# One-hots moved to VectorE and maxima spread with fewer products, in a graph attention layer on one core

## The chip, the cores and the metric

The kernel runs on one NeuronCore of one Trainium2 chip. The metric is the device time of one execution in microseconds (us), the median over several runs; lower is better. The engines have their own instruction streams, which meet at semaphores: PE (TensorE, matrix products, whose weight loads the profile lists as PEld), DVE (VectorE), ACT (ScalarE), POOL (GpSimd) and SP (SyncE, used here to start DMAs). Each executes its instructions in the order of the program.

## What is computed

A layer of relational graph attention with 5 relations, 8 heads of 16 and 3125 nodes of 128 features, over 100,000 edges that come sorted by their destination, followed by two residual layer norms. Cut to what matters:

```python
for r in range(R):                                   # R = 5 relations
    mask = edge_types == r
    q = einsum('eh,khd->ekd', x[dst], W_Q[r])
    k = einsum('eh,khd->ekd', x[src], W_K[r])
    v = einsum('eh,khd->ekd', x[src], W_V[r])
    logits = (q * k).sum(-1) / 4 + attn_bias[r]
    masked = where(mask, logits, -1e9)
    max_v = maximum(segment_max(masked, dst), -1e9)
    exp_l = where(mask, exp(masked - max_v[dst]), 0)
    sum_exp = segment_sum(exp_l, dst)
    attn = exp_l / (sum_exp[dst] + 1e-12)
    out = out + segment_sum(attn[:, :, None] * v, dst)
h = layernorm(x + out @ out_proj_w.T + out_proj_b)   # with gamma and beta
return layernorm(x + h)                              # without
```

The maximum of each node, relation and head must be known before the exponentials of that node's edges, which is what gives the kernel its two passes over the edges.

## The kernel before

**Tiles.** The edges are cut into 196 groups of 512 edges (`NGR`, `GE`): T = 4 tiles of 128 edges, one edge to a partition. Because the edges are sorted, the destinations of a group fall into a window of 25 nodes, that is WR = 125 pairs of node and relation.

**Before the loop** the keys and values of all nodes and relations are computed and stored to a table in DRAM (`kv_d`), the queries to another (`q_d`, written as three bf16 parts whose sum is the float32 value), and the indices are prepared.

**The loop** runs over steps k. An edge group passes it twice. On its first pass it is called g, one group a step from step 0 to 195:

- `gather(g)` (L681): four indirect DMAs issued by POOL fetch the key and value rows of the 512 edges from `kv_d` into one of 21 row buffers (`KVB`; group g overwrites group g - 21). It is issued two steps ahead (`AHEAD`). The gathers of groups 0 to 8 are issued before the loop.
- `fetch_keys`, `fetch_q` (L367, L373, SP): the keys `kt` of the edges' destinations, and the window's queries `qw`.
- `spot(g)` (L738): one tensor_scalar compares `kt` with the partition's number and writes the one-hot matrix `hot`, 125 x 512 in bf16. It stands two steps ahead of the group's own step. It runs on POOL, except for groups 0 and 1, which run on DVE.
- `spread_q(g)` (L747, PE): 12 products (4 tiles, 3 parts) with `hot` as weights bring each edge its query row, in PSUM.
- `logits(g)` (L760, L761, DVE): keys times queries, summed over each head; `store_logits` (L766, SP) writes them to DRAM.
- The logits of full blocks of 128 nodes are fetched again by one gather of POOL (`maxima_load`, L773, every eighth step), and `maxima` (L796 to L832, DVE, three steps in a row) takes the maximum of each node, relation and head. The result is again written as three bf16 parts, to `m_d`.

On its second pass, 16 to 19 steps later, the group is called v:

- `fetch_m(v)` (L854, SP): the maxima of the window, `mw`, 125 rows of 2 halves x 3 parts x 4 heads.
- `spread_m(v, times)` (L864, PE): 12 products with the same `hot` bring each edge the maxima of its destination, adding the three parts in PSUM. The row of maxima is repeated `times` times in each product, 8 while there are still gathers and 12 in the last 19 steps; only the first copy is read.
- `less_max(v)` (L873, DVE): logits less maxima, in place in PSUM (`mde`). `exps` (L877, ACT): the exponentials, in place. `weigh(v)` (L882, DVE): values times weights to `wv`, read from the row buffer and `mde`; `weights` (L890, ACT) copies the weights beside them.
- `places` (L902, L905, ACT): a second matrix `at` of 0 and 1, by destination.
- `sums(v, done)` (L916, L918, L925, PE): sums over the edges of each node and relation, with what the group before has left of a shared window (`carry`, L931, ACT), and, for a group two steps older, the sum over the relations (`by_node`, L950, ACT).
- `norm(v)` (L937 to L940, DVE): division by the sum of the weights.

Every block of 128 nodes then passes the output projection and the two norms (L957 to L1008).

**The order** is written out by hand in the loop of L1063 to L1155. Within a step DVE executes weigh(v) of the step, then `less_max` of the next group, `norm` of the group two steps older, `logits(g)`, then (for groups 0 and 1) `spot`, then queries and maxima, then the norms of nodes. POOL executes the four gathers of group k + 2, the gather of maxima when one is due, then `spot` of group k + 2. PE executes `spread_m` of the next group, `sums`, then `spread_q` of the next group. The `hot` tiles live in 21 buffers, `mw` in 4, `me` and `qe` in 2 banks of PSUM each.

Of the kernel before, what the change touches and what calls it, by code (L numbers as in the profile page):

```python
# [8 lines left out]
F32 = mybir.dt.float32  # L9
# [3 lines left out]
ALU = mybir.AluOpType  # L13
AX = mybir.AxisListType
# [3 lines left out]
P = 128  # L18
# [4 lines left out]
HEADS = 8  # L23
# [17 lines left out]
T = GE // P  # L41
# [5 lines left out]
WR = WN * R  # L47
# [67 lines left out]
def block_of(g, ends=tuple(P * (b + 1) for b in range(NT))):  # L115

    return min(
        b for b, n in enumerate(ends)
        if n >= N or E // N * n - slack(n) >= min(E, (g + 1) * GE)
    )  # L120
# [12 lines left out]
def windowed_path(  # L133
# [4 lines left out]
    nc = tc.nc  # L138
# [90 lines left out]
    def iota(name, pattern, n, base=0, mult=0, dt=F32, pool=const):  # L229
        t = pool.tile([P, n], dt, name=name)  # L230
        nc.gpsimd.iota(
            t, pattern=pattern, base=base, channel_multiplier=mult,
            allow_small_or_imprecise_dtypes=True,
        )
        return t

    node = iota("node", [[P, NT]], NT, mult=1)
    row_of = iota("row_of", [[0, 1]], 1, mult=1)
# [113 lines left out]
    live = {}  # L352
# [12 lines left out]
    def fetch_keys(g):  # L365
        kt = ahead.tile([P, T, P], BF16, name="kt")
        nc.sync.dma_start(kt.rearrange("w t p -> w (t p)"), key_d[g].partition_broadcast(P))  # L367
        live["kt", g] = kt

    def fetch_q(g):  # L370
        qw = ahead.tile([P, 3, H], BF16, name="qw")
        f = window(g, first5, SPE)
        nc.sync.dma_start(qw.rearrange("w s h -> w (s h)"), q_d[bass.ds(f, P), :])  # L373
        live["qw", g] = qw
# [298 lines left out]
    ps = ctx.enter_context(tc.tile_pool(name="ps", bufs=2, space=PSUM))  # L673
    buffers(i for i in range(KVB) if i not in at_once)
    hold = ctx.enter_context(tc.tile_pool(name="hold", bufs=HELD))
    flow = ctx.enter_context(tc.tile_pool(name="flow", bufs=2))
# [10 lines left out]
    def fetch_x(name, b):  # L687
        n = min(P, N - b * P)
        xb = flow.tile([P, H], F32, name=name, bufs=2 if name == "xq" else 3)
        if n < P:  # L690
            nc.vector.memset(xb, 0.0)
        nc.sync.dma_start(xb[:n], x[b * P : b * P + n, :])
        live[name, b] = xb
# [26 lines left out]
    def second_part():  # L720
        rem, q3 = live["rem"]
        nc.scalar.copy(q3[:, :, 1, :], rem)
# [5 lines left out]
    def store_q(b):  # L728
        live.pop(("xT", b))
        nc.sync.dma_start(  # L730
            q_d[b * P * R : (b + 1) * P * R, :].rearrange("(p r) c -> p (r c)", r=R),
            live.pop(("q3", b)).rearrange("p r s h -> p (r s h)"),
        )

    def spot(g):
        hot = hold.tile([WR, T, P], BF16, name="hot")
        on = nc.vector if g < 2 else nc.gpsimd
        on.tensor_scalar(hot, live.pop(("kt", g))[:WR], row_of[:WR], None, op0=ALU.is_equal)  # L738
        live["hot", g] = hot

    def spread_q(g):
# [109 lines left out]
    def fetch_m(g):  # L851
        mw = late_flow.tile([P, 2, 3, HEADS // 2], BF16, name="mw", bufs=4)
        f = window(g, first5, SPE)
        nc.sync.dma_start(mw.rearrange("w h s k -> w (h s k)"), m_d[bass.ds(f, P), :])  # L854
        live["mw", g] = mw


    def spread_m(g, times):

        me = ps.tile([P, T, times, 2, HEADS // 2], F32, name="me", tag="me")  # L860
        hot, mw = live.pop(("hot", g)), live.pop(("mw", g))
        for t in range(T):
            for s in range(3):
                nc.tensor.matmul(  # L864
                    me[:, t], hot[:, t, :],
                    mw[:WR, None, :, s, :].to_broadcast([WR, times, 2, HEADS // 2]),
                    start=(s == 0), stop=(s == 2),
                )
        live["mde", g] = me[:, :, 0].rearrange("p t h k -> p t (h k)")

    def less_max(g):
        mde = live["mde", g]
        nc.vector.tensor_tensor(mde, live.pop(("lg", g))[:, :, :HEADS], mde, op=ALU.subtract)  # L873

# [73 lines left out]
    def by_node(g):  # L948
        f = window(g, first, ACTE)
        nc.scalar.copy(oT[:, bass.ds(f, WN)], live.pop(("op", g)))  # L950
# [18 lines left out]
    def residual(b):  # L969
        n = min(P, N - b * P)  # L970
        if ("mv", b) not in live:
            live["mv", b] = pair()
            nc.vector.memset(live["mv", b], 0.0)
        xb = live["xr", b]
        nc.vector.tensor_tensor(xb[:n], xb[:n], beta_t[:n], op=ALU.add)
        h = late_flow.tile([P, H], F32, name="h", bufs=3)
        nc.vector.tensor_tensor(h[:n], live.pop(("pj", b))[:n], xb[:n], op=ALU.add)
        moments(live["mv", b][:, 0, :], h[:n], n)
        live["h", b] = h
# [34 lines left out]
    def store_z(b):  # L1014
        n = min(P, N - b * P)
        nc.sync.dma_start(out[b * P : b * P + n, :], live.pop(("z", b))[:n, :])
# [6 lines left out]
    group_at = {k: g for g, k in step_of.items()}  # L1023
# [10 lines left out]
    at_k, k = {}, 0  # L1034
    for v in range(NGR):
        k = max(k + 1, ready[block_of(v, MEND)])
        at_k[v] = k
    v_at = {k: v for v, k in at_k.items()}
# [24 lines left out]
    for k in range(-2, root_at[NT] + 2):  # L1063
        v, g = v_at.get(k), group_at.get(k)
        q_step = {k - f: b for b, f in enumerate(q_from) if b >= QB and -2 <= k - f <= 5}

        if k >= 0 and k + 3 in group_at:
            fetch_keys(group_at[k + 3])
            fetch_q(group_at[k + 3])
        if -2 in q_step:  # L1070
            fetch_x("xq", q_step[-2])
        for b in range(NT):
            if done_at[b] - 1 == k:
                fetch_x("xr", b)
            if norm_at[b + 1] + 1 == k:
                store_z(b)
        if 5 in q_step:
            store_q(q_step[5])
        for u in range(NGR):
            if max(at_k[u] - 3, ready[block_of(u, MEND)] - 2) == k:  # L1080
                fetch_m(u)

        for b in range(NT):
            if done_at[b] + 1 == k:
                residual(b)
        if v_at.get(k - 4) is not None:
            by_node(v_at[k - 4])
        if v_at.get(k - 2) is not None:
            carry(v_at[k - 2])
        if 1 in q_step:  # L1090
            turned(q_step[1])
        if 3 in q_step or 4 in q_step:
            second_part()
        if 2 in q_step or 3 in q_step:
            first_part()

        if v_at.get(k + 1) is not None:
            spread_m(v_at[k + 1], 8 if k + 1 in group_at else 12)
        if v_at.get(k - 1) is not None or v_at.get(k - 3) is not None:
            sums(v_at.get(k - 1), v_at.get(k - 3))  # L1100
        if k + 1 in group_at:
            spread_q(group_at[k + 1])

        if v is not None:
            weigh(v)
        while gathered < NGR - 1 and step_of[gathered + 1] <= k + AHEAD:
            gathered += 1
            gather(gathered)
        for b in range(NM):
            if full_step[b] + 1 == k:  # L1110
                maxima_load(b)
        if v_at.get(k + 1) is not None:
            less_max(v_at[k + 1])
            exps(v_at[k + 1])
        if v is not None:
            weights(v)
        if k + 1 in group_at:
            types(group_at[k + 1])
        if v_at.get(k - 2) is not None:
            norm(v_at[k - 2])  # L1120
        if g is not None:
            logits(g)
            store_logits(g)
        if k + 2 in group_at:
            spot(group_at[k + 2])
        if v_at.get(k + 1) is not None:
            places(v_at[k + 1], 2 if k >= final - 1 else 0)
        if 3 in q_step or 4 in q_step:
            third_part()
        if 2 in q_step or 3 in q_step:  # L1130
            remainder()
        for b in range(NM):
            whole = MB[b][2] is None
            last = ready[b] - (3 if whole else 4)
            if last - 2 == k and whole:
                maxima(b, 0, 2)
            if last - 1 == k and whole:
                maxima(b, 2, 4)
            if last == k:
                maxima(b, 4 if whole else 0, R)  # L1140
                store_m(b)
        for b in range(NT):
            if done_at[b] == k:
                project(b)
        for b in range(NT + 1):
            if root_at[b] == k:
                roots(b)
            if norm_at[b] == k:
                norms(b)
        if 0 in q_step:  # L1150
            turn_q(q_step[0])
        if 1 in q_step:
            queries(q_step[1], 0, RH)
        if 2 in q_step:
            queries(q_step[2], RH, R)  # L1155
# [505 lines left out]
```

## Time and profile before

| | us |
|---|---|
| runs | 1504.70, 1506.07, 1506.73 (median 1506.07) |
| the profiled execution | 1506.07 |
| its span (first to last instruction) | 1504.3 |
| busy in the span: PE, DVE, ACT, POOL | 1005.8, 901.7, 637.9, 1123.9 |

The mean granted clock of PE is 0.686 of full speed. What the program does when: the setup up to 93 us, gathers of POOL from 93.1 to 1419.1 with the loop, and the last steps, without gathers, to 1504.3.

How to read it: a line of a timeline gives the start in us, the duration in us, the engine, the source line, the operation with output and inputs, how many instructions run together, and in brackets the idle time of the engine ahead of it with what ended it. A line of the groups gives the busy time and mean duration in ns, then the idle time ahead of the group with its main cause; "issue" is time in which the engine waited for nothing that the profile shows. A line of the slices gives the busy share in tenths for each fortieth of the span. A line of the windows gives a stretch, its length, the busy time and count for PE, PEld, DVE, ACT and POOL, then the granted clock, the share of the DMA engines that was busy, and GB/s.

### The profile page before, as it was taken

Reading aid. Unit: us, or ns where it says so; the run is one execution under the profiler, and the core shown is the slowest. Engines: PE = TensorE matmul, PEld = TensorE weight load, DVE = VectorE, ACT = ScalarE, POOL = GpSimd, SP = SyncE. Lnnn points to the kernel's source line nnn. Section 1 sums busy time; section 2 is a strip of 40 time slices with the busy share of each in tenths; the row PEclk is TensorE's granted clock in tenths of the full one; section 3 lists DMA queues with packets and bytes.
Section 4 is the critical chain, followed back from the end, with each engine's and each line's share of the span. In section 5 each row is a group of like instructions: output and inputs, shape, how many; then the busy total and the mean of one; then the engine's idle time right before and its main releaser. Section 6 shows DMA issues by size and latency. Waiting matters only on the chain.

```text
span 1504.3 us, 26147 instructions
## 1 busy us (share of the span) xinstructions
PE 1005.8 (67%) x7526; PEld 800.1 (53%) x7526; DVE 901.7 (60%) x2365; ACT 637.9 (42%) x2248; POOL 1123.9 (75%) x1095
## 2 busy tenths in 40 slices
PE   7961336576676767667677677666776767667775
PEld 3530235455565645556565555555655555556664
DVE  5531446366557666656756665665765665566486
ACT  2540123344444454544544454444445444444354
POOL 2446788888888888888888888888888888888600
PEclk9975556566566677666767766767666776755688
DMA  6873544554554554455555545455545545444300
GB/s 184 317 255 96 143 132 122 141 139 119 146 135 128 141 139 127 132 148 128 126 146 136 127 140 140 122 145 138 135 125 144 137 125 142 130 132 120 98 17 16
DMA packets 180892, 203.66 MB, mean 135 GB/s; under 512 B 83207, under 2 KB 146083, under 8 KB 180620
## 3 DMA queue, kind: packets, MB, share of 16 engines
q0 software_dynamic: 40896, 113.39, 26.5%
q1 hardware_dynamic: 135414, 83.80, 22.7%
q10 hardware_dynamic: 4430, 4.71, 1.3%
q8 instruction: 63, 1.03, 0.3%
q14 instruction: 89, 0.73, 0.2%
HBM read 166.50 MB, written 35.28 MB: 134 GB/s over the span
## 4 chain that ended last, share of the span: by engine, by line
POOL 36%; PE 26%; issue 15%; DVE 11%; DMA 7%; another core or an unknown queue 2%; SPq 1%; ACT 1%; DVEq 0%; POOLq 0%; ACTq 0%
POOL kv L681 22%; POOL hot L738 14%; PE qe L747 6%; PE pp L916 6%; PE me L864 5%; DMA kv<-kv_d,idx 5%; PE pr L395 3%; DVE lg L761 2%; DVE prod L760 1%; PE prq L707 1%; PE pp L918 1%; PE pp L925 1%; DMA mw<-m_d 1%; POOL ell L773 1%
## 5 line engine op out<-in xcount | busy, mean ns | idle before, releaser
L681 POOL DMA_INDIRECT kv<-kv_d,idx x784 | 761.4, 971 | 227.6 <-issue 172.0
L747 PE MATMUL qe<-qw,hot 125*128 125x128 bf16 x2352 | 248.9, 283 | 435.1 <-POOL hot L738 393.1
L747 PEld LDWEIGHTS <-hot 125*128 125x128 bf16 x2352 | 202.8, 130 | 461.1 <-POOL hot L738 424.1
L916 PE MATMUL pp<-wv,at 128*125 128x136 f32 x1568 | 407.1, 402 | 0.0
L916 PEld LDWEIGHTS pp<-wv,at 128*125 128x125 f32 x1568 | 312.3, 272 | 69.4 <-issue 69.1
L738 POOL TENSOR_SCALAR hot<-kt,row_of 125x512 bf16<-125x512 bf16 x194 | 308.9, 1592 | 14.3 <-DMA kt<-key_d 8.4
L873 DVE TENSOR_TENSOR me<-lg,me 128x32 f32<-128x32 f32 x196 | 38.3, 195 | 357.0 <-PE pp L916 135.5
L877 ACT ACTIVATE me<-me 128x32 f32<-128x32 f32 x196 | 35.7, 182 | 486.2 <-issue 332.2
L902 ACT ACTIVATE at<-row_at,nkey 128x125 f32<-128x125 f32 x744 | 237.5, 398 | 0.0
L760 DVE TENSOR_TENSOR prod<-kv,qe 128x512 f32<-128x512 f32 x196 | 132.9, 678 | 63.5 <-PE qe L747 25.4
L864 PE MATMUL me<-mw,hot 125*128 125x64 bf16 (+1 forms) x2352 | 149.3, 229 | 24.9 <-DMA mw<-m_d 14.9
L864 PEld LDWEIGHTS <-hot 125*128 125x128 bf16 x2352 | 137.0, 123 | 51.5 <-issue 36.5
L882 DVE TENSOR_TENSOR wv<-kv,me 128x512 f32<-128x512 f32 x196 | 132.8, 677 | 23.2 <-remote 14.0
L761 DVE TENSOR_REDUCE lg<-prod 128x32 f32<-128x512 f32 x196 | 134.4, 686 | 6.7
L905 ACT ACTIVATE at<-at 128x500 f32<-128x500 f32 (+1 forms) x196 | 117.3, 599 | 6.2
L918 PE MATMUL pp<-pt,carried 125*5 125x136 f32 x390 | 100.7, 351 | 1.1 <-ACT pt L931 0.9
L811 DVE TENSOR_TENSOR wl<-by_head,shut 128x1024 f32<-128x1024 f32 (+2 forms) x73 | 76.9, 1053 | 12.7 <-ACT by_head L788 10.2
L925 PEld LDWEIGHTS pp<-rsum,o 125*128 125x128 f32 x392 | 80.9, 250 | 4.2 <-issue 4.1
L817 DVE TENSOR_REDUCE mx<-wl 128x16 f32<-128x1024 f32 (+2 forms) x73 | 76.5, 1048 | 2.5
L925 PE MATMUL pp<-rsum,o 125*128 125x25 f32 x392 | 71.6, 266 | 4.0 <-DVE o L940 4.0
L950 ACT COPY oT<-pp 128x25 f32 x196 | 33.8, 172 | 86.4 <-remote 32.1
L395 PE MATMUL pr<-wkv,xT 128*128 128x512 f32 x150 | 60.8, 547 | 3.6 <-issue 3.1
(185 smaller groups left out, 987.3 us busy)
## 6 DMA issues: line engine op xcount, KB each, us to landing
kt<-key_d SPq DMA_DIRECT2D x196, 128.0 KB
qw<-q_d SPq DMA_DIRECT2D x196, 96.0 KB
kv_d<-kvs SPq DMA_DIRECT2D x24, 640.0 KB
kv<-kv_d,idx POOLq DMA_INDIRECT x784
q_d<-q SPq DMA_DIRECT2D x22, 480.0 KB
lg_d<-lg SPq DMA_DIRECT2D x196, 18.0 KB
mw<-m_d SPq DMA_DIRECT2D x196, 6.0 KB
xr<-in_x SPq DMA_DIRECT2D x24, 64.0 KB
```

The lines of the kernel that those rows point to most:

```text
L681: nc.gpsimd.indirect_dma_start(out=kv[:, t, :], out_offset=None, in_=kv_d[:, :], in_offset=bass.IndirectOffsetOnAxis(ap=idx[:, t, g : g + ...
L738: on.tensor_scalar(hot, live.pop(("kt", g))[:WR], row_of[:WR], None, op0=ALU.is_equal)
L747: nc.tensor.matmul(qe[:, t, :], hot[:, t, :], qw[:WR, s, :], start=(s == 0), stop=(s == 2))
L760: nc.vector.tensor_tensor(prod, kv[:, :, :H], live.pop(("qe", g)), op=ALU.mult)
L761: nc.vector.tensor_reduce(lg[:, :, :HEADS], prod.rearrange("p t (k d) -> p t k d", d=HD), AX.X, ALU.add)
L864: nc.tensor.matmul(me[:, t], hot[:, t, :], mw[:WR, None, :, s, :].to_broadcast([WR, times, 2, HEADS // 2]), start=(s == 0), stop=(s == 2),)
L882: nc.vector.tensor_tensor(wv[:, :, :H].rearrange("p t (k d) -> p t k d", d=HD), kv[:, :, H:].rearrange("p t (k d) -> p t k d", d=HD), live ...
L902: nc.scalar.activation(at[:, t, :], row_at[:, :WR], AF.Abs, bias=nkey[:, t, g : g + 1], scale=1.0)
L905: nc.scalar.activation(at[:, on_dve:], at[:, on_dve:], AF.Relu, bias=1.0, scale=-1.0)
L916: nc.tensor.matmul(pp, at[:, t, :], wv[:, t, :], start=(t == 0), stop=(t == T - 1))
L918: nc.tensor.matmul(pp[:R], carried[:WR, g, :], live.pop(("pt", g - 1)), start=False, stop=False,)
L925: nc.tensor.matmul(op, live.pop(("o5", done)), rsum[:WR], start=True, stop=True)
```

## The change

Two things are changed. All of `spot` runs on DVE. And while there are gathers, `spread_m` issues one product for each of the four tiles instead of three: the three parts stand side by side in the product's columns, repeated 5 times (5 x 24 = 120 columns), and `less_max` first adds the three parts with a tensor_reduce on DVE into a new tile in SBUF, which the subtraction, the exponentials, `weigh` and `weights` then use in place of PSUM. In the last 19 steps the 12 products stay.

```diff
     def spot(g):
         hot = hold.tile([WR, T, P], BF16, name="hot")
-        on = nc.vector if g < 2 else nc.gpsimd
-        on.tensor_scalar(hot, live.pop(("kt", g))[:WR], row_of[:WR], None, op0=ALU.is_equal)
+        nc.vector.tensor_scalar(hot, live.pop(("kt", g))[:WR], row_of[:WR], None, op0=ALU.is_equal)
         live["hot", g] = hot

     def spread_m(g, times):

+        hot, mw = live.pop(("hot", g)), live.pop(("mw", g))
+        if times < 8:
+            me = ps.tile([P, T, times, 2, 3, HEADS // 2], F32, name="me", tag="me")
+            for t in range(T):
+                nc.tensor.matmul(
+                    me[:, t], hot[:, t, :],
+                    mw[:WR, None].to_broadcast([WR, times, 2, 3, HEADS // 2]),
+                    start=True, stop=True,
+                )
+            live["parts", g] = me[:, :, 0].rearrange("p t h s k -> p t h k s")
+            return
         me = ps.tile([P, T, times, 2, HEADS // 2], F32, name="me", tag="me")
-        hot, mw = live.pop(("hot", g)), live.pop(("mw", g))
         for t in range(T):
             for s in range(3):
                 nc.tensor.matmul(
...
     def less_max(g):
+        if ("parts", g) in live:
+            mde = flow.tile([P, T, 2, HEADS // 2], F32, name="mde")
+            nc.vector.tensor_reduce(mde, live.pop(("parts", g)), AX.X, ALU.add)
+            live["mde", g] = mde.rearrange("p t h k -> p t (h k)")
         mde = live["mde", g]
         nc.vector.tensor_tensor(mde, live.pop(("lg", g))[:, :, :HEADS], mde, op=ALU.subtract)
...
         if v_at.get(k + 1) is not None:
-            spread_m(v_at[k + 1], 8 if k + 1 in group_at else 12)
+            spread_m(v_at[k + 1], 5 if k + 1 in group_at else 12)
```

## The prediction

> **What bounds the kernel now.** I read the busy shares and the slices first, then the costliest groups, then the timeline of one stretch of POOL, then the windows by stage.
>
> ```profile
> PE 1005.8 (67%) x7526; PEld 800.1 (53%) x7526; DVE 901.7 (60%) x2365; ACT 637.9 (42%) x2248; POOL 1123.9 (75%) x1095
> POOL 2446788888888888888888888888888888888600
> ```
>
> ```profile
> L681 POOL DMA_INDIRECT kv<-kv_d,idx x784 | 761.4, 971 | 227.6 <-issue 172.0
> L747 PE MATMUL qe<-qw,hot 125*128 125x128 bf16 x2352 | 248.9, 283 | 435.1 <-POOL hot L738 393.1
> L738 POOL TENSOR_SCALAR hot<-kt,row_of 125x512 bf16<-125x512 bf16 x194 | 308.9, 1592 | 14.3 <-DMA kt<-key_d 8.4
> L873 DVE TENSOR_TENSOR me<-lg,me 128x32 f32<-128x32 f32 x196 | 38.3, 195 | 357.0 <-PE pp L916 135.5
> ```
>
> POOL is the busiest engine and flat at 8 tenths from slice 8 to the end of the loop; PE's largest wait is for POOL's hot. The stretch of POOL shows why it is not 10 tenths:
>
> ```profile
> 198.67 1.00 POOL L681 DMA_INDIRECT kv<-kv_d,idx  x1 [0.17 <-issue]
> 199.97 0.97 POOL L681 DMA_INDIRECT kv<-kv_d,idx  x1 [0.31 <-issue]
> 201.25 0.95 POOL L681 DMA_INDIRECT kv<-kv_d,idx  x1 [0.30 <-issue]
> 202.51 0.95 POOL L681 DMA_INDIRECT kv<-kv_d,idx  x1 [0.30 <-issue]
> 203.49 1.59 POOL L738 TENSOR_SCALAR hot<-kt,row_of 125x512 bf16<-125x512 bf16 x1
> 205.25 1.00 POOL L681 DMA_INDIRECT kv<-kv_d,idx  x1 [0.17 <-issue]
> ```
>
> The 0.3 us between gathers is issue, no wait. From the first gather of one step to that of the next: 205.25 - 198.67 = 6.58 us. Every eighth step a gather of maxima (L773) adds 0.96 + 0.31 = 1.27, or 0.16 a step: 6.74. Gathers 0 to 8 are issued before the loop; the train of gather 9 starts at 157.9, and 157.9 + 187 x 6.74 = 1418.3, against 1419.1 read for the end of the last gather. So POOL's program is the whole time to there; the drained pipeline behind it takes 85 us. The profiled execution is 1506.07 (span 1504.3, 1.8 around it), which is the median of the runs too, so the sum needs no shift.
>
> The stage windows bound the other engines:
>
> ```profile
> 600.00:1000.00 400.00, 279.18 (x2200) 228.22 (x2197) 251.43 (x659) 188.31 (x660) 331.43 (x304) 0.68 0.53 136
> 1420.00:1504.00 84.00, 56.65 (x512) 45.88 (x512) 62.27 (x231) 37.42 (x151) 2.96 (x3) 0.81 0.09 20
> ```
>
> In 400 us, 59.3 steps of 6.74: PE 4.71 us a step at a granted clock of 0.68, DVE 4.24, ACT 3.17.
>
> **A second thing that POOL does to the loop.** Two pairs of lines, the first from the steady part, the second from the end, where no gathers run:
>
> ```profile
> 766.70 0.85 PE L864 MATMUL me<-mw,hot 125*128 125x64 bf16 x12
> 769.13 0.20 DVE L873 TENSOR_TENSOR me<-lg,me 128x32 f32<-128x32 f32 x1 [3.15 <-PE pp L916]
> ...
> 1452.40 0.68 PE L864 MATMUL me<-mw,hot 125*128 125x96 bf16 x12 [0.36 <-DMA mw<-m_d]
> 1453.18 0.20 DVE L873 TENSOR_TENSOR me<-lg,me 128x32 f32<-128x32 f32 x1 [0.59 <-PE me L864]
> ```
>
> DVE is idle in both, yet its subtraction begins 769.13 - 767.55 = 1.6 us after the last product of maxima in the first (median over the loop 1.6) and 0.1 in the second. So PE's finished signals come late while a train of four gathers is issued; many of them come together some 0.9 us after the last gather of a train, that is, during the hot. Before the loop, where gathers run back to back with no hot between, it is far worse:
>
> ```profile
> 105.63 2.72 PE L747 MATMUL qe<-qw,hot 125*128 125x128 bf16 x24 [1.47 <-issue]
> ...
> 118.58 0.69 DVE L760 TENSOR_TENSOR prod<-kv,qe 128x512 f32<-128x512 f32 x1 [12.79 <-issue]
> ...
> 143.77 0.69 DVE L760 TENSOR_TENSOR prod<-kv,qe 128x512 f32<-128x512 f32 x1 [23.78 <-remote]
> ```
>
> The products of groups 0 and 1 are done at 107.1 and 108.35; their consumers start at 118.6 and at 143.8, 5 us after the last gather of that train (its last began at 137.49). The cause of the delay isn't visible, its size is.
>
> **The change, part by part.**
>
> *The hot moves from POOL to DVE.* POOL loses 194 instructions; a step's train becomes 4 x 1.26 = 5.04 us (137.49 - 136.23 = 1.26 in the run without hots), with maxima 5.20: 1.54 us less a step. On DVE the same instruction took 353 and 456 ns in its two cases (groups 0 and 1), 0.36 from start to start at most; bounds 0.2 (the small tensor_scalar L806, median 194 ns) and 1.59 (POOL's own price). I take 0.36, the same instruction. It issues no DMA. On DVE it stands behind logits(k), which waits for qe(k), and ahead of the maxima, queries and weigh(k+1); PE's spread_q(k+2) and, sixteen or so steps later, spread_m wait for it. It no longer waits for POOL's train, so the 393.1 us that PE idles for it go.
>
> The Trainium skill ("SBUF — State Buffer", Who interferes with whom) has a rule against this: a tensor_scalar on DVE in a two-port mode locks the port pair that it shares with GpSimd, and whoever issues second waits in full. The row that bears on it is L806, a tensor_scalar run beside the gathers, at 182 to 490 ns; by the rule 187 hots of 0.36 us would give 67 us back to POOL, which I leave out of the sum.
>
> *The spread in 4 products.* 12 products of 64 columns (L864 mean 229 ns, a group of 12 taking 0.52 us warm and 0.85 cold from start to end) become 4 of 120 columns; nearest row L747, 128 columns, 283 ns: a third of a 12-group that takes 0.84 to 1.46, so 0.28 to 0.49. PE gets 0.25 to 0.35 us shorter a step in 177 steps and issues 56 instead of 72 matmuls and weight loads. PE isn't the bound, so this is worth nothing on the path by itself: its cover is the 435.1 us of idle ahead of L747. If that cover goes, it is worth the 0.3. Its other side is the clock: less work may keep the clock at half. At half clock the step's products take 0.49 + 1.70 + 0.6 + 0.82 + 0.46 + 1.46 = 5.5 us.
>
> *The sum of three parts.* One tensor_reduce of 96 elements a partition more on DVE, 32 out; bounds L873 (195 ns, 32 elements) and L761 (686 ns, 512 elements); 96 is nearer to 32, so 0.2, ahead of the subtraction, and thus on the chain me, less_max, exps, weigh. PSUM's me is free once it is summed, instead of after weigh and weights: no wait for it shows now, so nothing.
>
> DVE comes to 4.24 + 0.36 + 0.20 = 4.8 us a step, under 5.20.
>
> *Where the stall goes.* gather(k+2) overwrites the rows that weigh(k) reads (21 buffers, group g over g-21). Now weigh ends 1.6 to 29 us before the gather that it lets go, 5.8 at the median. At 1.54 us saved a step, that reserve is spent within four steps; from there POOL waits for weigh. Weigh waits for exps, they for less_max, it for a signal of PE, and that signal comes late in a train. Without the hot there is no gap behind a train, so POOL runs two trains (one has its weigh done already), stops, and only this stop lets PE's signals through. The stop: 0.9 us until the signals come, then DVE's chain from less_max through norm and logits to the end of weigh, 763.25 to 765.98 in the timeline, 2.73 us: together 3.6 for two trains, 1.8 a step. Bounds: 0.9 + 0.68 (weigh alone behind the signal) = 1.6, or 0.8 a step; and 3.6 + 0.56 (hot and sum) + 1.35, or 2.75 a step. (1.35: DVE's 4.24 less the 2.89 that its seven instructions of every step take by their rows leaves 1.35 a step for maxima, queries and norms, 2.7 in two steps, of which I let half fall into the stop.) I take 1.8: in the lines above less_max itself is what comes late.
>
> **Sum of the forecast.** Gathers 9 to 20 overwrite nothing: 12 steps at 5.20 instead of 6.74, -18.5. The other 175 go at 5.20 + 1.80 = 7.00 instead of 6.74: +45.5. 1506.1 - 18.5 + 45.5 = 1533 us. With a stop of 1.55 a step, 1489; with 2.45, 1647: that is its own range.
>
> **Rivals.**
> 1. *POOL bounds as it does now, and gets shorter.* For: the flat slices, and the reserve ahead of each gather. Against: the two consumers that started 11.5 and 35 us late. 157.9 + 187 x 5.20 = 1130, + 85 + 1.8: 1217; with DVE or a cold PE as the bound (5.5 us a step) 1273.
> 2. *A short stop.* The signal of maxima comes at the end of the third gather, as at 769.13, since now 8 instead of 24 instructions of PE stand behind it; behind the stop comes weigh alone. 0.8 a step: 6.0, 1367; 1.35 a step, 6.55, 1470. For: 16 instructions fewer to be signalled. Against: without the gap, 24 products were enough for the delay of 11.5 us.
> 3. *Slower*, my forecast's mechanism: place, the lack of a gap behind each train; price, the stop; it decides from a stop of 1.64 us a step, where -18.5 + 175 x (5.20 + stop - 6.74) is zero. At the upper bound of 2.75 it gives 1506.1 - 18.5 + 175 x 1.21 = 1699.
> 4. *The hot on DVE takes what it took on POOL*, 1.59: DVE at 6.03 a step, 1372. No row on DVE comes near.
>
> **How the numbers follow.** The forecast's case 0.56 (slower 0.50, within 0.03, faster 0.03), the short stop 0.27 (faster 0.24, within 0.02, slower 0.01), POOL, DVE or PE as the bound 0.15, the rest 0.02, slower. About 0.2% is what a measurement of this kernel can tell from no change. Faster 0.42, same 0.05, slower 0.53. The likeliest time is 1533. For 8 in 10 the range leaves out the POOL-bound case and the top of the stop: 1367 to 1650.
>
> **What would show it.** Right: gathers in pairs of trains with a stop of 3 to 4 us before the third, first gather of a pair released by weigh (L882); L873's place taken by the reduce, waiting on PE with 2 us and more between me's last product and it; L738 on DVE at 0.36. Wrong: trains without stops at 5.04, or stops under 2 us; a reduce that starts 0.1 us after its products; hots on DVE of over 1 us, or gathers whose 0.96 grows beside them.

## The result, and the profile after

| | before | after |
|---|---|---|
| median, us | 1506.3 (1504.7 to 1506.7) | 1556.8 (1549.2 to 1564.8) |
| ratio | | 1.034 (95% interval 1.028 to 1.039) |
| profiled span, us | 1504.3 | 1551.9 |
| granted clock of PE | 0.686 | 0.708 |

The change makes the kernel 3.4% slower. 1533 was forecast, in a range of 1367 to 1650. In what follows a *train* is the four gathers of one group, a *row* is what POOL issues without a stop, and a *stop* is a wait of POOL ahead of a train. First the page of the profile after: the busy times, POOL's slices, and the groups that answer to those shown of before (idle time and its main cause behind the last bar; "remote" is a wait whose end the profile can put down to no instruction of this core).

```profile
PE 912.1 (59%) x6110; PEld 690.0 (44%) x6110; DVE 972.3 (63%) x2736; ACT 648.0 (42%) x2248; POOL 808.4 (52%) x901
POOL 2556354464655655565565566556556455555500
...
L681 POOL DMA_INDIRECT kv<-kv_d,idx x784 | 753.5, 961 | 552.3 <-DVE mde L883 302.2
L746 PE MATMUL qe<-qw,hot 125*128 125x128 bf16 x2352 | 230.8, 260 | 107.5 <-issue 63.2
L883 DVE TENSOR_REDUCE mde<-me 128x32 f32<-128x96 f32 x177 | 44.7, 253 | 260.2 <-remote 146.6
```

POOL has lost 315 us of work and is no longer flat. PE has lost nearly all of its wait for the hot. In their place POOL waits 302 us ahead of gathers. DVE waits 260 us ahead of the sum of the maxima, where it waited 357 us ahead of the subtraction before. The windows, with the columns as before (PE, PEld, DVE, ACT, POOL, clock, DMA share, GB/s):

```profile
600.00:1000.00 400.00, 234.16 (x1660) 180.45 (x1658) 269.70 (x760) 185.54 (x644) 228.54 (x238) 0.72 0.52 131
...
1465.00:1551.00 86.00, 61.49 (x538) 49.85 (x535) 66.89 (x244) 40.61 (x164) 5.20 (x6) 0.80 0.11 24
```

No engine is over 68% busy in the middle: the engines wait for each other. What they wait for shows in the timeline. First PE's products and the consumer on DVE at the end of a row of gathers that ran from 683.36 to 699.72 with no stop (POOL's lines are further down):

```profile
692.45 0.44 PE L746 MATMUL qe<-qw,hot 125*128 125x128 bf16 x5
693.39 0.39 PE L746 MATMUL qe<-qw,hot 125*128 125x128 bf16 x2 [0.50 <-issue]
694.09 0.27 PE L746 MATMUL qe<-qw,hot 125*128 125x128 bf16 x1 [0.32 <-issue]
694.81 0.38 PE L746 MATMUL qe<-qw,hot 125*128 125x128 bf16 x2 [0.46 <-issue]
696.22 0.37 PE L746 MATMUL qe<-qw,hot 125*128 125x128 bf16 x2 [1.02 <-issue]
...
701.25 0.26 DVE L883 TENSOR_REDUCE mde<-me 128x32 f32<-128x96 f32 x1 [9.97 <-remote]
```

The twelve products are one group, which in the kernel before takes 0.84 us where the granted clock is 1.0 and 1.46 where it is 0.5. Here, after the first five, they drip out one or two at a time, 0.7 us or a multiple of it apart, with nothing that the profile shows to wait for. The products that this sum reads were done at 688.1 (their group starts at 687.74 and takes 0.37), and the sum begins at 701.25, 1.5 us after the last gather. So the row of gathers delays PE's signals, as the prediction said, and in the end PE's own instructions too, which it had not said. Of the groups of queries from group 14 on, 18 of 182 took over 1.8 us, up to 8.0; before, none took over 1.46. From group 52 on all 15 of these are eight groups or a multiple of eight apart, so they keep to the eight-step round of the maxima; which part of that round sets them off isn't shown.

The same round on POOL:

```profile
683.36 0.95 POOL L681 DMA_INDIRECT kv<-kv_d,idx  x1 [3.49 <-DVE mde L883]
...
698.77 0.95 POOL L681 DMA_INDIRECT kv<-kv_d,idx  x1 [0.30 <-issue]
706.31 0.95 POOL L681 DMA_INDIRECT kv<-kv_d,idx  x1 [6.59 <-DVE mde L883]
...
713.06 0.95 POOL L681 DMA_INDIRECT kv<-kv_d,idx  x1 [2.05 <-DVE mde L883]
```

A row of three trains, then a stop of 6.6 us, then single trains with stops of 1 to 2 us (a gather of maxima at 693.77 stands within the row). Each gather behind a stop starts 0.27 us after the end of the weigh that freed its buffer (the profile names the instruction next to it, L883); 109 of the 175 trains from group 21 on start within 0.5 us of that weigh, before none.

Last, the start, where no buffer has to be waited for:

```profile
155.35 0.69 DVE L759 TENSOR_TENSOR prod<-kv,qe 128x512 f32<-128x512 f32 x1 [31.87 <-remote]
...
223.09 0.69 DVE L759 TENSOR_TENSOR prod<-kv,qe 128x512 f32<-128x512 f32 x1 [28.34 <-remote]
```

```profile
150.53 0.94 POOL L681 DMA_INDIRECT kv<-kv_d,idx  x1 [0.30 <-issue]
175.97 0.94 POOL L772 DMA_INDIRECT ell<-lg_d,start_i  x1 [24.50 <-DMA kt<-key_d]
...
244.51 0.95 POOL L772 DMA_INDIRECT ell<-lg_d,start_i  x1 [22.60 <-DVE mde L883]
```

POOL gathers in two long rows, which end at 151.5 and 221.9; DVE stands still for 32 and 28 us, until 3.9 and 1.2 us after the end of each row; then POOL stands still for 24.5 and 22.6 us, since its next instruction, the gather of maxima (L772), needs the logits that DVE couldn't compute in the meantime.

### The profile page after: what moved, and what is told of

It reads as the page before. It is cut to its first block, busy times and chain, and to the rows that moved or that the text cites. A ratio compares the mean times of both kernels' runs of the same rounds, so it can differ in the third digit from the quotient of the medians.

```text
span 1551.9 us, 22874 instructions
## 1 busy us (share of the span) xinstructions
PE 912.1 (59%) x6110; PEld 690.0 (44%) x6110; DVE 972.3 (63%) x2736; ACT 648.0 (42%) x2248; POOL 808.4 (52%) x901
## 4 chain that ended last, share of the span: by engine, by line
DVE 32%; PE 21%; another core or an unknown queue 16%; issue 15%; DMA 5%; ACT 5%; SPq 3%; POOL 1%; DVEq 0%; ACTq 0%; POOLq 0%
PE pp L929 7%; DVE prod L759 4%; DVE wv L895 4%; DVE wl L810 4%; DVE lg L760 4%; PE qe L746 3%; DMA mw<-m_d 3%; PE pr L395 3%; PE me L863 3%; DVE mx L816 3%; ACT at L915 2%; PE pp L931 2%; DVE hot L737 2%; DVE mde L883 1%
## 5 line engine op out<-in xcount | busy, mean ns | idle before, releaser
L929 PE MATMUL pp<-wv,at 128*125 128x136 f32 x1568 | 380.3, 378 | 112.6 <-DVE o L953 52.8
L929 PEld LDWEIGHTS pp<-wv,at 128*125 128x125 f32 x1568 | 289.0, 252 | 192.7 <-issue 101.8
L746 PE MATMUL qe<-qw,hot 125*128 125x128 bf16 x2352 | 230.8, 260 | 107.5 <-issue 63.2
L746 PEld LDWEIGHTS <-hot 125*128 125x128 bf16 x2352 | 206.3, 127 | 119.8 <-issue 73.9
L890 ACT ACTIVATE mde<-mde 128x32 f32<-128x32 f32 x177 | 40.6, 229 | 487.1 <-DVE mde L886 346.6
L883 DVE TENSOR_REDUCE mde<-me 128x32 f32<-128x96 f32 x177 | 44.7, 253 | 260.2 <-remote 146.6
L895 DVE TENSOR_TENSOR wv<-kv,mde 128x512 f32<-128x512 f32 x177 | 120.5, 681 | 65.3 <-remote 58.3
L863 PE MATMUL me<-mw,hot 125*128 125x120 bf16 x708 | 90.8, 262 | 103.4 <-DMA mw<-m_d 70.7
L863 PEld LDWEIGHTS <-hot 125*128 125x128 bf16 x708 | 61.5, 120 | 136.4 <-DMA mw<-m_d 68.9
L707 PE MATMUL prq<-wq,xTq 128*128 128x384 f32 (+1 forms) x88 | 50.2, 666 | 112.2 <-DVE rem L717 107.9
L931 PEld LDWEIGHTS pp<-pt,carried 125*5 125x5 f32 x390 | 18.2, 86 | 206.1 <-ACT pt L944 94.2
```

The source lines that it names most:

```text
L746: nc.tensor.matmul(qe[:, t, :], hot[:, t, :], qw[:WR, s, :], start=(s == 0), stop=(s == 2))
L863: nc.tensor.matmul(me[:, t], hot[:, t, :], mw[:WR, None].to_broadcast([WR, times, 2, 3, HEADS // 2]), start=True, stop=True,)
L895: nc.vector.tensor_tensor(wv[:, :, :H].rearrange("p t (k d) -> p t k d", d=HD), kv[:, :, H:].rearrange("p t (k d) -> p t k d", d=HD), live ...
L929: nc.tensor.matmul(pp, at[:, t, :], wv[:, t, :], start=(t == 0), stop=(t == T - 1))
L931: nc.tensor.matmul(pp[:R], carried[:WR, g, :], live.pop(("pt", g - 1)), start=False, stop=False,)
```

## The experiments

Two theories went into them. The *gap theory*: PE's signals pass when POOL issues no gather, and the hot on POOL was a gap of that kind behind every train. The *DVE theory*: the loop is slowed by the 0.6 us that hot and sum add to DVE's chain, and POOL's order doesn't matter. Where the table or the text says "gap", it is the smallest time from the end of a train's last gather to the next gather (in e8 from its second to its third); many trains of the runs with 0.30, and of e12, wait longer all the same.

| run | hots on | products | behind each train | gap, us | median, us | ratio to before (95%) |
|---|---|---|---|---|---|---|
| before | POOL | 12 | the hot | 1.79 | 1506 | |
| after | DVE | 4 | nothing | 0.30 | 1557 | 1.034 (1.028, 1.039) |
| e1 | DVE | 12 | nothing | 0.30 | 1639 | 1.084 (1.078, 1.090) |
| e2 | POOL | 4 | the hot | 1.79 | 1526 | 1.009 (1.006, 1.013) |
| e3 | DVE | 4 | 512 columns, unused | 1.79 | 1542 | 1.020 (1.016, 1.023) |
| e4 | DVE | 4 | 256 columns, unused | 1.15 | 1433 | 0.949 (0.946, 0.951) |
| e5 | DVE | 4 | 128 columns, unused | 0.83 | 1345 | 0.894 (0.891, 0.896) |
| e6 | half each | 4 | half the hot | 1.15 | 1408 | 0.934 (0.932, 0.937) |
| e7 | DVE | 4 | no gathers from group 21 | | 1239 (one run) | |
| e8 | DVE | 4 | 256 columns, amid the train | 1.15 | 1402 | 0.932 (0.929, 0.934) |
| e9 | DVE | 4 | 16 columns, unused | 0.54 | 1305 | 0.867 (0.866, 0.869) |
| e10 | POOL 1/4 | 4 | a quarter of the hot | 0.83 | 1351 | 0.898 (0.897, 0.900) |
| e11 | DVE | 12 | 128 columns, unused | 0.83 | 1324 | 0.881 (0.879, 0.882) |
| e12 | DVE | 12 | 16 columns, unused | 0.54 | 1574 | 1.046 (1.044, 1.048) |

Ratios are against the kernel before, run beside it on the same chip (1504 to 1511 us; the runs are from several chips).

**e1 and e2: each half of the change alone.** e1 is the kernel before with the one line of `spot`; e2 is the changed kernel with the old two lines.

```diff
-        on = nc.vector if g < 2 else nc.gpsimd
-        on.tensor_scalar(hot, live.pop(("kt", g))[:WR], row_of[:WR], None, op0=ALU.is_equal)
+        nc.vector.tensor_scalar(hot, live.pop(("kt", g))[:WR], row_of[:WR], None, op0=ALU.is_equal)
```

> The kernel before with only the hots moved to DVE (12 products stay). Gap theory (PE's signals pass when POOL issues no gather, and the hot was such a gap behind every train): slower than before, 1540 to 1620, trains in uneven rows with stops, since 72 PE instructions a step have to be signalled instead of 56. DVE theory (the hot and the sum lengthen DVE's chain, POOL's order doesn't matter): only the hot's 0.35 us of the 0.6 us is added, so about 0.35/0.6 of the way from 1506 to 1557: 1530 to 1540.

> The kernel before with only the 4 products and the sum on DVE (hots stay on POOL). Gap theory: POOL's cadence of 6.58 us holds, so 1495 to 1515, no change. DVE theory: 0.25 us a step on DVE's chain in 177 steps, 1515 to 1550.

e1 took 1639, more than either theory gave it and a hundred us more than the DVE theory allows: it does less on DVE than the changed kernel and is 82 us slower. It issues 72 instead of 56 matmuls and weight loads a step. So moving the hot costs 128 us by itself (1639 - 1511 on that chip), and the 4 products give most of that back. e2 took 1526, above the gap theory's range and inside that of the DVE theory. POOL's order holds in it (no train is released by weigh), but 0.9% is lost all the same: 15 us between the medians on that chip, 20 us between the profiled spans (1524.5, and 1504.3 on another chip). Below, these are compared with what POOL's own instructions take longer.

**e3, e4: the gap put back, the work not.** POOL executes an instruction of the hot's form into a tile that nobody reads; DVE goes on making the hots. The two tiles that it uses are left out here.

```diff
+    def rest():
+        nc.gpsimd.tensor_scalar(
+            spare[:WR, :512], still[:WR, :512], row_of[:WR], None, op0=ALU.is_equal
+        )
...
             spot(group_at[k + 2])
+            if group_at[k + 2] >= 2:
+                rest()
```

> The changed kernel, and POOL executes behind each train an instruction of the hot's form and size into a tile that nobody reads; DVE still makes the hots. Gap theory: POOL's 1.55 us a step come back and the time still falls, to 1495 to 1520, with even trains at 6.58 us. DVE theory: 1557 or more, since nothing is taken from DVE.

> As the run before, with an instruction of half the columns, so a gap of some 0.8 to 1.0 us behind each train. Gap theory: if 0.9 us is what the signals need, trains at about 6.0 us and 1380 to 1450; if it isn't enough for weigh to be through, stops remain and 1450 to 1540. DVE theory: 1557.

e3 gives POOL 1.59 us of useless work a step and is still 15 us faster than the changed kernel, with no train released by weigh any more; e4, with half of it, is 5% faster than before. Nothing was taken from DVE in either. The DVE theory falls: it gave 1557 or more for both. But e3 missed its range (1495 to 1520), by a loss like that of e2.

**e5, e6, e8, e9, e10: how long a gap, and where.** The rest with 128 and 16 columns; in e8 the rest of 256 between the second and the third gather; in e6 and e10 a useful rest, the first two tiles or the first tile of the hot (e8's edit first, then e6's; groups 0 and 1 stay whole on DVE):

```diff
+            if g >= KVA and t == 1:
+                rest()
...
-        nc.vector.tensor_scalar(hot, live.pop(("kt", g))[:WR], row_of[:WR], None, op0=ALU.is_equal)
+            nc.gpsimd.tensor_scalar(hot[:, :2], kt[:WR, :2], row_of[:WR], None, op0=ALU.is_equal)
+            nc.vector.tensor_scalar(hot[:, 2:], kt[:WR, 2:], row_of[:WR], None, op0=ALU.is_equal)
```

> The changed kernel with an unused POOL instruction of 128 columns behind each train, so a gap of about 0.8 us from the end of the last gather to the next (with 256 columns 1.15, without any 0.30). Gap theory: if the signals need 0.9 us after the last gather, this gap is too short, rows of trains with stops come back and the time is 1470 to 1557; if any gap will do, trains of 5.8 to 6.0 us and 1370 to 1410. DVE theory, in what is left of it after the rest of 256 columns gained: 1400 to 1440 whatever the gap.

> The changed kernel with the hot divided: tiles 0 and 1 on POOL behind the train, tiles 2 and 3 on DVE. The gap behind each train is useful work of 0.95 us, and DVE's hot becomes shorter. Gap theory: as with the rest of 256 columns or a little better, 1400 to 1440. DVE theory: the hot's DVE price halves, so 1557 - 30 = 1525.

> The changed kernel with the rest of 256 columns between the second and the third gather of each train instead of behind the fourth: as many gathers in a row and as long a gap, at another place in the step. Gap theory: 1410 to 1450, as behind the train. If the gap works only because it comes right ahead of the gather that waits for weigh: stops remain, 1480 to 1560.

> The changed kernel with an unused POOL instruction of 16 columns behind each train, a gap of about 0.55 us (0.83 us with 128 columns gave 1345, 0.30 without any gave 1557). If the gap's length decides and 0.55 is too short: rows of trains with stops, 1400 to 1557. If any POOL instruction between trains is enough: trains at 5.3 + 0.35 = 5.65 us, 1285 to 1320.

> The changed kernel with the hot divided: tile 0 on POOL behind the train (a gap of 0.83 us that does useful work), tiles 1 to 3 on DVE. Gap theory: 1335 to 1355, as with the unused instruction of 128 columns. If a shorter hot on DVE gains by itself: under 1335.

The shorter the gap, the faster, down to 0.54 us: 1542, 1433, 1345, 1305. e5 is faster than any of its expectations had it (the lowest was 1370), and e8 is 8 us under its range; e6, e9 and e10 are inside. So the idea that the signals need 0.9 us of quiet is wrong: with 4 products 0.54 us behind the train is enough, and so is a break amid the train (e8). Each of these breaks is an instruction of POOL; whether a pause without one would do isn't shown. POOL in e9:

```profile
701.76 0.35 POOL L683 TENSOR_SCALAR spare<-still,row_of 125x16 bf16<-125x16 bf16 x1
702.27 1.00 POOL L690 DMA_INDIRECT kv<-kv_d,idx  x1 [0.17 <-issue]
703.58 0.97 POOL L690 DMA_INDIRECT kv<-kv_d,idx  x1 [0.30 <-issue]
704.86 1.07 POOL L690 DMA_INDIRECT kv<-kv_d,idx  x1 [0.31 <-issue]
706.23 0.95 POOL L690 DMA_INDIRECT kv<-kv_d,idx  x1 [0.30 <-issue]
707.21 0.35 POOL L683 TENSOR_SCALAR spare<-still,row_of 125x16 bf16<-125x16 bf16 x1
```

5.45 us from rest to rest, against 5.00 for a bare train, and the group of the sum over the whole run, which waited 260 us in the changed kernel:

```profile
L892 DVE TENSOR_REDUCE mde<-me 128x32 f32<-128x96 f32 x177 | 44.5, 251 | 48.2 <-PE me L872 47.0
```

Measured over groups 20 to 169, the time by which the first reader of the maxima starts after both its product's end and DVE's being free is 1.0 us at the mean before, 1.3 in the changed kernel, 2.1 in e1, and 0.02 in e5, e8 and e9. A useful rest is no better than a useless one (e10 1351, e5 1345; e6 1408, e8 1402), which fits that the hot's 0.34 us on DVE isn't on the path that sets the end.

e4 doesn't fit the order: it still has stops (17 trains released by weigh, 0.6 us of delay at the mean), though its gap lies between those of e3 and e5, and e6 and e8 have the same gap and none. Why is open.

**e7: is it the gathers?** Instead of the four gathers of groups 21 and on:

```diff
+            if g >= KVB:
+                nc.gpsimd.tensor_scalar(
+                    kv[:, t, :], wkv[:, t % R].rearrange("p a h -> p (a h)"), 1.0, None, op0=ALU.mult
+                )
+                continue
```

> The changed kernel in which groups from 21 on are not gathered: POOL writes their row buffers by four tensor_scalar instructions instead (logits and values are then those of a constant), with the same waits on weigh. It asks whether it is the issuing of gathers or any occupation of POOL that holds PE's signals back. If the issuing: no stops, the sum of parts begins 0.1 us after the last product of maxima, DVE or PE bounds the loop at 4.9 to 5.5 us a step, 1150 to 1290. If any occupation of POOL: stops of several us as in the changed kernel, 1450 or more.

1239 us, inside the first range. With POOL writing for 3.5 us a step (four instructions of 0.87 us at the mean) and waiting for weigh as ever, the first reader is 0.02 us late at the mean, and no group of queries takes over 1.49 us. It isn't POOL's being occupied. But the run takes the gathers' traffic away as well as their issue, and doesn't tell these two apart; e9, which has all of that traffic in less time (159 GB/s at 600 to 1000 us, against 131) and none of the delay, speaks against the traffic.

**e11, e12: and PE's share in it.** The kernel before with the hots on DVE, thus 12 products, and the two short rests.

> The kernel before with the hots on DVE and an unused POOL instruction of 128 columns behind each train, 12 products a step, no sum on DVE. If the number of PE's instructions to be signalled (72 a step instead of 56) matters only where trains run in rows: POOL bounds it at 5.9 us a step, 1325 to 1350. If the gap of 0.83 us lets only so many through: stops, 1400 to 1550, and the 4 products are worth the difference.

> The kernel before with the hots on DVE, 12 products a step and an unused POOL instruction of 16 columns behind each train. With 128 columns, 12 products took 1324 and 4 products 1345; with 16 columns 4 products took 1305. If POOL bounds it and the sum on DVE is what costs the 20 us: 1280 to 1295. If PE's 72 instructions a step meet the signals' limit again at this gap of 0.55 us: stops, over 1320.

e11 took 1324.5, half a us under the range that was expected without stops (1325 to 1350). e12 fell off: 1574, slower than before, with a POOL instruction of 0.34 us behind every train. Its timeline, in the middle of the loop, has PE dripping as in the changed kernel:

```profile
707.03 0.48 PE L755 MATMUL qe<-qw,hot 125*128 125x128 bf16 x3 [0.68 <-issue]
707.76 0.26 PE L755 MATMUL qe<-qw,hot 125*128 125x128 bf16 x1 [0.25 <-issue]
708.48 0.48 PE L755 MATMUL qe<-qw,hot 125*128 125x128 bf16 x3 [0.46 <-issue]
710.59 0.37 PE L755 MATMUL qe<-qw,hot 125*128 125x128 bf16 x2 [1.62 <-issue]
711.33 0.37 PE L755 MATMUL qe<-qw,hot 125*128 125x128 bf16 x2 [0.37 <-issue]
...
711.51 0.20 DVE L881 TENSOR_TENSOR me<-lg,me 128x32 f32<-128x32 f32 x1 [9.38 <-remote]
```

So a gap of 0.54 us is enough for 56 instructions of PE a step (e9, 1305) and not for 72 (e12, 1574), and one of 0.83 is enough for 72 (e11, 1324). These runs fit a limit on how many of PE's instructions pass in a step, which depends on the gap and, where it is met, costs the loop some 250 us. The limit itself isn't measured, and e4's stops, at 56 instructions and 1.15 us, don't fit it.

**The loss of e2 and e3.** This part is argued from rows of the runs above; no run keeps the sum in PSUM. e11 is 21 us faster than e5, with 12 products instead of 4, and e2's span is 20 us longer than that of before. The sum's tile is in SBUF, and with it `weigh` and the subtraction read both inputs from SBUF; with 12 products one of them is in PSUM. From e5, a gather beside weigh, and then the subtraction beside the end of that gather:

```profile
729.13 0.66 DVE L904 TENSOR_TENSOR wv<-kv,mde 128x512 f32<-128x512 f32 x1
729.30 1.31 POOL L690 DMA_INDIRECT kv<-kv_d,idx  x1 [0.30 <-issue]
729.71 0.25 DVE L892 TENSOR_REDUCE mde<-me 128x32 f32<-128x96 f32 x1
730.00 0.44 DVE L895 TENSOR_TENSOR mde<-lg,mde 128x32 f32<-128x32 f32 x1
```

The gather takes 1.31 us, not 0.95, and the subtraction 0.44, not 0.19. What POOL's gathers and hots take beyond their medians sums up to 10.6 us before and 28.5 us in e2 (from 230 us on); the difference of 17.9 stands against 20.2 between the two spans. In e3 it is 40.5, and its span is 34.9 longer than before. In e5 it is 32, in e11 18, a difference of 14 against 17 between the spans. Of the 30 gathers of e3 that take over 1.15 us, 28 stand beside a weigh and 5 beside a hot. Of the gathers beside a weigh, 41 of 194 take that long in e5, but 4 of 192 in e11 and 1 of 186 before, where weigh reads one input from PSUM. The Trainium skill ("SBUF — State Buffer", Who interferes with whom) says that a DVE instruction with two SBUF inputs contends with a GpSimd instruction that reads SBUF; the rows agree. The same section infers that a tensor_tensor doesn't hold up descriptor generation; here the gather beside weigh took 0.36 us more, and the measurement decides.

## Why the prediction was right, and where it wasn't

The time is made of three stretches: 239.6 to 247.6 us for the start of the train of group 21 (+8.0), 174 steps from there at 6.99 us instead of 6.75 (+41.9), and 87.8 instead of 90.0 us from the start of the last train to the end (-2.2): +47.7, against 47.6 between the spans. The forecast had -18.5, +45.5 and 0.

- *What bounds the kernel before: POOL's program.* Right. e9 has the same gathers with 0.35 us behind them in place of 1.59, and ends 200 us earlier.
- *The hot on DVE, 0.36 us.* Right: 344 ns at the median. It is not what costs; e10 and e5 differ by 6 us. The rule on the two-port mode that was weighed against it doesn't show in the changed kernel: a gather beside a hot takes 0.95 us at the mean, as without one. With rests it shows a little: in e11, 17 of the 59 rests that stand beside a hot take over 0.08 us more than the median rest, and none of the others.
- *The sum, 0.2 us.* 0.25. As a term of DVE's time right, DVE 4.65 us a step (399 us in 600 us of 85.8 steps), 4.8 forecast. But its tile in SBUF goes with a loss of POOL time, 18 us in e2, for which the prediction had no term.
- *4 products, nothing on the path by themselves.* Wrong once trains run bare or nearly so: 82 us between e1 (12) and the changed kernel (4), 269 between e12 and e9. The 0.3 us a step that the prediction allowed if PE's cover goes would be 53 us in 177 steps.
- *Trains of 5.04 us, stops of 1.80 a step.* 5.00 (four gathers 1.25 apart), or 5.16 with the maxima, and 6.99 - 5.16 = 1.83, of which stops ahead of gathers are 1.71. The mechanism holds: with a break in each row and nothing taken from DVE, the stops go (e3, e5, e8; e4 keeps some). The closeness of the two numbers is partly luck, as the form differs. It was not pairs of trains with 3.6 us behind them, but rows of one (65), two (27) and more trains (17) with stops of up to 9.8 us between them. 45 of the 109 stops are under 2 us, which the prediction had named as a sign of being wrong; in these DVE is idle for only 7 of 67 us, so they are DVE's order: at 713.06 weigh had stood behind the hot and the maxima, from 708.3 to 712.1. In the 64 longer ones DVE is idle for 84 of 265 us. The 0.9 us that the prediction let pass until the signals come has no row in the steady loop of before: there the subtraction starts, at the median, 1.2 us ahead of the end of the nearest train.
- *The start, -18.5 us.* This is the step that failed: +8.0. "Gathers 9 to 20 overwrite nothing" is so, but POOL's queue also holds the gathers of maxima, which wait for logits, and the bare rows of the start hold these up by 32 and 28 us. The train of group 9 starts 21 us earlier than before and that of group 21 8 us later, so the twelve trains between took 110.8 us instead of 81.7. The prediction had shown the lines of just such a delay (143.77, idle 23.78), and priced the start without it. The 26.5 us between forecast and measurement here are more than the whole miss of the profiled execution (20.7); the loop and the drain give 6 us back.
- *The rivals.* POOL as the bound (1217) and the short stop (1367 to 1470) did not come. With a POOL instruction of 0.35 us behind each train the changed kernel takes 1305 us and its trains hardly stop (e9). The short stop's two times don't follow the prediction's own sum, which gives 1358 and 1454 for 0.8 and 1.35 us a step: they use the shorter step for all 187 trains.

What the runs show is that uninterrupted rows of gathers hold up PE's signals and then PE, and with which gaps 4 and 12 products run without it. Through which path the gathers do so isn't shown.

## What to carry to other kernels

Ask of an instruction on a busy engine not only what it costs but what it separates: here 1.59 us of work on the bounding engine was also the only break between bursts of DMA issue: with 12 products, removing it whole cost 128 us (e1), and putting 0.62 us in its place gained 180 (e11). Look for a consumer that starts long after its producer's end while its engine is idle, compare it with a stretch in which the suspected neighbour is silent, and put an empty instruction there before moving real work. Where an operand moves from PSUM to SBUF, look at what POOL does beside its readers.

## What was not expected of the hardware

- Held up by a row of gathers, PE issues matrix products one to three at a time, about 0.7 us or a multiple of it apart (693.39, 694.09, 694.81, 696.22). After the row the next group of twelve takes 1.18 us, and the one of 687.07, early in the row, had taken 0.83.
- It looks like a cliff: 0.83 to 0.54 us of gap takes 12 products from 1324 to 1574 us, and 4 products from 1345 to 1305. No run lies between the two gaps.
- The best run, e9, is the changed kernel plus an instruction of 16 columns whose result nobody reads: 1305 us, 13% faster than before. With 12 products it was 5% slower than before, so at that gap the gain needs the 4 products.
